# A graph network kernel with a hand-written issue order: block work spread over iterations, weight scaling on ScalarE, thresholds on GpSimd, single PSUM banks

## The chip, the cores and the metric

One core of one Trainium2 chip. The metric is the device time of one execution in microseconds; lower is better. Every kernel timed here gave a correct result. All medians and ranges quoted are of runs labelled "fast". Three kernels had one run each labelled "slow", being over 1.5% above the fastest of the same kernel; it is left out. Engines are named as in the profile: PE is TensorE, PEld its weight loads, DVE is VectorE, ACT is ScalarE, POOL is GpSimd.

## The reference

128 graphs of 64 nodes with 128 features. For every edge (i, j) of the adjacency matrix a three-layer perceptron runs on the pair of features; the messages are summed by node and a second perceptron updates the node.

```python
def _mlp(x, w0, b0, g0, be0, w1, b1, g1, be1, w2, b2):
    h = _layernorm(relu(x @ w0 + b0), g0, be0)
    h = _layernorm(relu(h @ w1 + b1), g1, be1)
    return h @ w2 + b2

messages = _mlp(concat(f_i, f_j), msg_...) * adj[..., None]     # (128, 64, 64, 128)
agg      = sum(messages, axis=2)
updated  = x + _mlp(concat(x, agg), upd_...)                    # cut: names shortened
```

About an eighth of the pairs are edges, so the kernel packs the edges first. It works in 160 iterations of 512 edges; ten iterations are one block of eight graphs, and four of ten iterations also sum a pair of graphs.

## The kernel before

"Node marks" are five matmuls that write a 128x128 tile each into PSUM; each half of a tile is then scaled by the reciprocal standard deviation of its edges (the "weights"), and `reduce` uses them as the stationary operand.

```python
ps_z = es.enter_context(tc.tile_pool(name="ps_z", bufs=2, space=PSUM))
ps_y = es.enter_context(tc.tile_pool(name="ps_y", bufs=1, space=PSUM))
ps_m = es.enter_context(tc.tile_pool(name="ps_m", bufs=2, space=PSUM))
def bank():
    return ps_m.tile([P, 512], F32, name="ms")
# ... (cut)
def make_tp(p):
    tp = tpp.tile([P, CAP], F16, name="tp")
    nc.vector.tensor_scalar(tp, slot, cumall[:, p:p + 1], None, op0=ALU.is_lt)
# ... (cut)
def weights(p):
    q, h = divmod(p, 2)
    w = wp.tile([P, TG, 2, N], F32, name="w")
    qv = Q[q][:, h * 2 * TG:(h + 1) * 2 * TG].rearrange("p (g t) -> p t g", g=2)
    for t0, t1 in ((0, CH), (CH, TG)):
        ps = bank()
        for t in range(t0, t1):
            nc.tensor.matmul(ps[:, (t - t0) * P:(t - t0 + 1) * P],
                             lhsT=TP[p][:, t * P:(t + 1) * P],
                             rhs=pick.rearrange("p g m -> p (g m)"), start=True, stop=True)
        nt = t1 - t0
        nc.vector.tensor_tensor(w[:, t0:t1], ps[:, 0:nt * P].rearrange(...),
                                qv[:, t0:t1].unsqueeze(3).to_broadcast([P, nt, 2, N]),
                                op=ALU.mult)                       # cut: one argument shortened
```

PSUM is the memory that the matmuls write to. A tile of 512 f32 columns in it is called a bank here; a pool with `bufs=2` has two banks and hands them out anew when they have been read.

Names in the profile, in the order of the work: `tp` are the thresholds and `mk` the marks of the edges, which the compare turns into the selection `s`; `hps` and `h` are the first layer, `hT` is h transposed for its statistics `st`; `z` is the second layer's product, `sdb` what is added to it, `y` its output; `w` are the weights and `ys` the sum over edges. `um...`, `uh`, `uy` and `usdb` are their counterparts in the update of the nodes, `xn` and `ysum` its inputs; `abh` and `abl` are a high and a low part of the first layer's products by node.

Marks and weights stand in one function, so a bank is filled and read at once. The block's other work (transposes, layer products of the update) comes from generators that a scheduler interleaves.

## Time and profile before

| | before |
|---|---|
| median of 3 runs, first measurement | 772.11 us |
| span of the profiled run, mean granted clock | 769.7 us, 0.956 |
| PE busy, DVE busy | 654.7 us (85%), 673.4 us (87%) |
| one block (ten iterations), from the y rows | 44.3 us |

"Busy" is the union of an engine's instructions. The mean granted clock is the share of full speed at which TensorE was let run. The lines behind these numbers stand in the prediction.

### The profile page before, as it was taken

To read this page: it belongs to the slowest core of one execution; us is meant where nothing else is said; L and a number is where in the kernel's file an instruction comes from. 1 tells how busy PE (TensorE), PEld (TensorE's weight loads), DVE (VectorE), ACT (ScalarE), POOL (GpSimd) and SP (SyncE) were. 2 spreads that over 40 slices of the span, in tenths; PEclk is the share of its full clock that TensorE was granted. 3 is DMA by queue.
4 is the path that set the end of the run, shared out by engine and by line. 5 is a ranking of instruction groups with operands and counts; after the bars stand their busy time and mean duration, and the time that the engine had idled before them with its cause. 6 is when DMAs were issued, how large, how long until landed. Compare 5 with 4: busy or idle time off the path is not lost.

```text
span 769.7 us, 15357 instructions
## 1 busy us (share of the span) xinstructions
PE 654.7 (85%) x5667; PEld 558.6 (73%) x5667; DVE 673.4 (87%) x2397; ACT 208.0 (27%) x402; POOL 366.1 (48%) x651
## 2 busy tenths in 40 slices
PE   2688899898898979889898988889799898989773
PEld 2567778687777868778786877778687787878663
DVE  7678998988888999898998989989989898999872
ACT  1143232232232223223322323222232233222111
POOL 6346345444354454545455454545545354435531
PEclk9699999999899999999999999989999999999997
DMA  5000000100001010000101000010000000000000
GB/s 137 1 21 8 3 8 1 35 1 24 12 2 36 1 30 7 15 22 1 35 3 35 1 17 14 1 29 1 29 1 16 1 1 14 1 15 2 14 15 16
DMA packets 27883, 12.04 MB, mean 16 GB/s; under 512 B 10391, under 2 KB 27805, under 8 KB 27805
## 3 DMA queue, kind: packets, MB, share of 16 engines
q1 hardware_dynamic: 26496, 11.01, 5.1%
q8 instruction: 46, 0.75, 0.4%
q14 instruction: 33, 0.26, 0.1%
q10 hardware_dynamic: 1308, 0.01, 0.1%
HBM read 6.82 MB, written 4.19 MB: 14 GB/s over the span
## 4 chain that ended last, share of the span: by engine, by line
PE 48%; DVE 36%; POOL 10%; issue 2%; ACT 2%; DMA 1%; ACTq 0%; POOLq 0%; DVEq 0%
PE z L435 8%; PE ys L476 7%; DVE st L446 7%; PE ms L504 7%; PE hps L410 7%; DVE s L401 7%; PE hT L420 5%; DVE st L424 5%; PE mk L396 4%; PE ms L358 3%; DVE y L234 3%; POOL xo L488 3%; PE ms L494 2%; DVE uo L538 2%; POOL sdb L429 2%
## 5 line engine op out<-in xcount | busy, mean ns | idle before, releaser
L429 POOL TENSOR_TENSOR sdb<-b1b,m_sd 128x512 f32<-128x512 f32 x160 | 168.1, 1052 | 194.4 <-DVE y L234 136.0
L435 PE MATMUL z<-w1c,h 128*128 128x128 f32 x1280 | 201.3, 288 | 2.9 <-DVE y L234 2.5
L413 ACT ACTIVATE h<-hps,b0c 128x512 f32<-128x512 f32 x160 | 110.1, 688 | 311.8 <-PE hps L410 308.4
L435 PEld LDWEIGHTS z<-w1c,h 128*128 128x128 f32 x1280 | 173.4, 197 | 16.0 <-DVE y L234 7.6
L424 DVE BATCH_NORM_STATS2 st<-hT 128x6 f32<-128x128 f32 x640 | 147.4, 283 | 4.1 <-PE hT L420 3.9
L446 DVE BATCH_NORM_STATS2 st<-y 128x6 f32<-128x128 f32 x640 | 137.4, 278 | 0.0
L401 DVE TENSOR_TENSOR s<-mk,cmpt 128x512 fp32r<-128x512 f32 x160 | 109.4, 684 | 15.9 <-PE mk L396 14.8
L410 PE MATMUL hps<-s,abl 128*128 128x512 f32 (+3 forms) x256 | 101.9, 408 | 18.1 <-DVE s L401 17.7
L420 PE MATMUL hT<-ident,h 128*128 128x128 f32 x640 | 104.8, 288 | 6.6 <-DVE st L424 6.2
L234 DVE CUSTOM_DVE_ANT_0 y<-z,sdb 128x512 f32<-128x512 f32 x160 | 107.9, 676 | 1.3 <-POOL sdb L429 1.3
L396 PE MATMUL mk<-tp,qs 128*128 128x512 f16 (+3 forms) x256 | 66.4, 312 | 38.6 <-DVE s L401 30.1
L420 PEld LDWEIGHTS hT<-ident,h 128*128 128x128 f32 x640 | 75.2, 146 | 24.3 <-DVE st L424 18.7
L476 PE MATMUL ys<-y,w 128*64 128x128 f32 x1280 | 91.0, 281 | 1.8 <-DVE w L461 1.8
L476 PEld LDWEIGHTS ys<-y,w 128*64 128x64 f32 x1280 | 73.2, 139 | 14.9 <-issue 10.2
L410 PE MATMUL hps<-s,abh 128*128 128x512 f32 (+3 forms) x256 | 81.8, 336 | 0.0
L410 PEld LDWEIGHTS hps<-s,abl 128*128 128x128 f32 x256 | 51.6, 202 | 26.8 <-DVE s L401 20.2
L396 PEld LDWEIGHTS <-qs 128*128 128x128 f16 x256 | 25.1, 100 | 58.8 <-issue 57.0
L461 DVE TENSOR_TENSOR w<-ms,m_q 128x512 f32<-128x512 f32 (+1 forms) x128 | 61.0, 479 | 0.4 <-PE ms L456 0.4
L410 PEld LDWEIGHTS hps<-s,abh 128*128 128x128 f32 x256 | 52.0, 203 | 0.9
L240 POOL TENSOR_TENSOR m_d<-st 128x20 f32<-128x20 f32 x64 | 15.9, 248 | 73.8 <-DVE st L424 52.1
L244 DVE SCALAR_TENSOR_TENSOR m<-m_d,m_s 128x20 f32<-128x20 f32 x64 | 11.5, 179 | 32.0 <-POOL m_d L241 29.9
L488 POOL TENSOR_TENSOR xo<-xn,cu2b 128x512 f32<-128x512 f32 x16 | 20.5, 1282 | 34.3 <-DVE uo L538 33.3
(162 smaller groups left out, 939.1 us busy)
## 6 DMA issues: line engine op xcount, KB each, us to landing
xn<-in_x_dram SPq DMA_DIRECT2D x16, 256.0 KB, 2.8
out_dram<-uo SPq DMA_DIRECT2D x16, 256.0 KB, 2.3
an<-in_adj_dram SPq DMA_DIRECT2D x16, 128.0 KB, 2.2
w<-in_L_gnn_msg_w_dram SPq DMA_DIRECT2D x2, 64.0 KB, 2.3
u<-in_L_gnn_upd_w_dram SPq DMA_DIRECT2D x2, 64.0 KB, 2.1
w0a<-in_L_gnn_msg_w_dram SPq DMA_DIRECT2D x1, 64.0 KB, 1.8
w0b<-in_L_gnn_msg_w_dram SPq DMA_DIRECT2D x1, 64.0 KB, 2.4
u0a<-in_L_gnn_upd_w_dram SPq DMA_DIRECT2D x1, 64.0 KB, 2.3
```

Of the source, the lines that this page charges most:

```text
L234: nc.vector._custom_dve(TENSOR_ADD_SAT, out=o, in0=ps, in1=sb, s0=BIG, s1=0.0)
L396: nc.tensor.matmul(ps[:, at:at + w], lhsT=blocks[g // (2 * PB)]["qs"][:, g // 2 % PB, g % 2, :], rhs=TP[g // 2][:, e:e + w], start=True, s ...
L401: nc.vector.tensor_tensor(s, ps, cmpt[:, o:o + CH * P], op=ALU.is_equal)
L410: nc.tensor.matmul(ps[:, at:at + w], lhsT=ab[:, g % 4, :], rhs=s[:, at:at + w], start=(k == 0), stop=(k == 1))
L413: nc.scalar.activation(h, ps, AF.Relu, bias=b0c)
L420: nc.tensor.transpose(ps[:, t, :], H[n][:, t * P:(t + 1) * P], ident)
L424: nc.vector.bn_stats(ST0[q][:, CH * c + t, :], ps[:, t, :])
L429: nc.gpsimd.tensor_tensor(sdb, bc(W["b1b"], CH), SD[q][:, CH * c:CH * c + CH].unsqueeze(2).to_broadcast([P, CH, C]), op=ALU.mult)
L435: nc.tensor.matmul(ps[:, t, :], lhsT=h[:, t * P:(t + 1) * P], rhs=W["w1c"], start=True, stop=True)
L446: nc.vector.bn_stats(ST1[q][:, CH * c + t, :], Y[n][:, t, :])
L461: nc.vector.tensor_tensor(w[:, t0:t1], ps[:, 0:nt * P].rearrange("p (t g m) -> p t g m", t=nt, g=2), qv[:, t0:t1].unsqueeze(3).to_broadcas ...
L476: nc.tensor.matmul(YS[b][g * N:(g + 1) * N, k, :], lhsT=w[:, t, g, :], rhs=y, start=(t == 0), stop=(t == TG - 1))
```

## The change

The intent: VectorE and TensorE were both nearly full, and TensorE could do its work in about 36 us per block. So VectorE is relieved (weights to ScalarE, thresholds and small variance steps to GpSimd), and each piece of block work gets a fixed iteration and place, in an order that the framework may not alter. The core of the diff, cut:

```diff
-        ps_z = es.enter_context(tc.tile_pool(name="ps_z", bufs=2, space=PSUM))
+        ps_z = es.enter_context(tc.tile_pool(name="ps_z", bufs=1, space=PSUM))
-        ps_m = es.enter_context(tc.tile_pool(name="ps_m", bufs=2, space=PSUM))
+        ps_a = es.enter_context(tc.tile_pool(name="ps_a", bufs=2, space=PSUM))   # abank(), "ma"
+        ps_u = es.enter_context(tc.tile_pool(name="ps_u", bufs=1, space=PSUM))   # ubank(), "mu"
-            nc.vector.tensor_scalar(tp, slot, cumall[:, p:p + 1], None, op0=ALU.is_lt)
+            nc.gpsimd.tensor_scalar(tp, slot, cumall[:, p:p + 1], None, op0=ALU.is_lt)
+        def node_marks(p):
+            WT[p] = []
+            for t in range(TG):
+                if t % 4 == 0:
+                    ps = abank()
+                WT[p].append(ps[:, t % 4 * P:(t % 4 + 1) * P])
+                nc.tensor.matmul(WT[p][t], lhsT=TP[p][:, t * P:(t + 1) * P], ...)
         def weights(p):
-                nc.vector.tensor_tensor(w[:, t0:t1], ps..., qv..., op=ALU.mult)
+            for t in range(TG):
+                for g in range(2):
+                    nc.scalar.activation(w[:, t, g, :], WT[p][t][:, g * N:(g + 1) * N], AF.Copy,
+                                         scale=Q[q][:, k:k + 1])
+            at(u - 1, "e", bias0, b)              # GpSimd, two instructions
+            at(u + 1, "x", turn, b, "ysum")       # PE: four transposes into abank()
+            at(u + 5, "a", upd_root0, b)          # ACT: um_sd, from a GpSimd result
+            at(u + 5, "x", turn, b, "uh")         # PE, abank()
+            at(u + 6, "a", turn_out, b, "uh")     # ACT copies that bank
+            at(u + 8, "x", turn, b, "uy")         # PE, abank()
+            at(w, "x", node_marks, p)             # PE fills two abanks
+            at(w + 1, "r", weights, p)            # ACT reads them, one iteration later
+            at(w + 2, "x1", reduce, p)
+        es.enter_context(tc.manual_schedule())
```

Within an iteration the places come in the order a, (compare, statistics), m, (layer 1, layer 0 with `h` on ACT), r, x, x1, x2, (marks of the next iteration), e.

## The prediction

> **What bounds the kernel now.** I read the page's busy shares first. Columns: busy us, share of the span, instructions.
>
> ```profile
> PE 654.7 (85%) x5667; PEld 558.6 (73%) x5667; DVE 673.4 (87%) x2397; ACT 208.0 (27%) x402; POOL 366.1 (48%) x651
> ```
>
> The shares include the start and the end, so next the table of stretches. Columns: stretch, span, then busy and count of PE, PEld, DVE, ACT, POOL, then the clock.
>
> ```profile
> 200.00:300.00 100.00, 88.65 (x791) 76.17 (x788) 89.50 (x322) 29.55 (x58) 47.87 (x86) 0.98 0.05 14
> 400.00:500.00 100.00, 87.90 (x784) 75.21 (x783) 92.11 (x337) 29.48 (x58) 50.81 (x93) 0.98 0.05 13
> ```
>
> VectorE (DVE) is over 90% busy on average and TensorE (PE) close to 90%: two engines are nearly full, each waiting for the other. Which of them is truly full, only a dense piece tells. PE, in the timeline (start, duration, operation):
>
> ```profile
> 421.65 0.60 PE L420 MATMUL hT<-ident,h 128*128 128x128 f32 x4
> 422.09 0.83 PE L435 MATMUL z<-w1c,h 128*128 128x128 f32 x6
> 422.76 0.60 PE L333 MATMUL ms<-pos,dq 128*128 128x256 f32 x2
> 423.29 1.31 PE L476 MATMUL ys<-y,w 128*64 128x128 f32 x20
> 424.53 0.66 PE L348 MATMUL ms<-ident,xn 128*128 128x128 f32 x4
> 425.03 0.38 PE L396 MATMUL mk<-tp,qs 128*128 128x512 f16 x1
> ...
> 425.76 0.62 PE L420 MATMUL hT<-ident,h 128*128 128x128 f32 x4
> ```
>
> From start to start: four transposes hT 0.44 us, a z pass 0.11, the dq product 0.53, a whole ys reduction 1.24, a block transpose 0.50, marks and both hps products together 0.73. Durations overlap; starts are what counts. Between such pieces PE waits for DVE, as the list of waits says (total, times, longest):
>
> ```profile
> PE mk L396 <- DVE s L401: 30.1, 43, 1.0
> PEld hT L420 <- DVE st L424: 18.7, 33, 1.5
> POOL sdb L429 <- DVE y L234: 136.0, 79, 3.5
> ```
>
> So DVE sets the pace and PE fills its gaps. A loop iteration handles 512 edges; there are 160, ten per block. The y rows of the timeline start at 90.5 us (the tenth) and 710.7 (the 150th): 44.3 us per block.
>
> **What the Trainium skill says.** "Trainium Kernel Development and Optimization", section Best Practices: judge TensorE not by matmul busy time. The trace agrees: six z passes "last" 0.83 us but the next work starts after 0.67. "GPSIMD Engine Reference", section 4.1: two-input elementwise work is about twice slower there than on VectorE, one-input work roughly at line rate, PSUM out of reach. The trace has 1052 ns for the two-input 512-column sdb and 615 ns for the f16 copy of 512; so the thresholds (one input, SBUF) can go to GpSimd, and the weights (PSUM) only to ScalarE. "VectorE: DVE Perf Modes", section What auto-detection actually checks: the packed mode wants every tensor 16-bit. In s the PSUM operand stays f32, so cmpt in f16 should leave s at its 684 ns. "PSUM — Partial Sum Buffer", section on bank collisions: guard by bank. With one z bank, z of the next iteration waits for y of this one; before, two banks hid that.
>
> **The change part by part.** Off DVE (lines of the groups by form: busy us, mean ns):
>
> ```profile
> L461 DVE TENSOR_TENSOR w<-ms,m_q 128x512 f32<-128x512 f32 x64 | 43.6, 681 | 0.4 <-PE ms L456 0.4
> L376 DVE TENSOR_SCALAR tp<-slot,cumall 128x640 f16<-128x640 f16 x64 | 26.3, 417 | 0.0
> L461 DVE TENSOR_TENSOR w<-ms,m_q 128x128 f32<-128x128 f32 x64 | 17.7, 276 | 0.0
> L314 DVE COPY deg<-rk 128x4 f32<-128x4 f32 x16 | 10.3, 644 | 0.0
> L244 DVE SCALAR_TENSOR_TENSOR m<-m_d,m_s 128x20 f32<-128x20 f32 x64 | 11.5, 179 | 32.0 <-POOL m_d L241 29.9
> ```
>
> That is 109 us; with the small variance steps and copies (L244 for blocks, L250, L258, L312, L343) about 137, or 8.5 per block; about 8 as a union. DVE then has per iteration, by starts, s 0.60, four statistics 0.80, y 0.60, four more 0.77 = 2.77, and per block 6.5 of other work: 34 us per block.
>
> PE does the same products: per iteration z 0.90, hT 0.44, marks and hps 0.75-0.8, say 2.15; per four graph pairs 4 x (1.24 + 0.30 for node marks) = 6.1; per block 8.2 (two row steps of 1.0, dq 0.5, counts 0.25, four transposes 1.8, 32 layer passes of 0.11). Sum 35.8 per block. A perfect schedule is therefore PE bound at 36 us against 44.3.
>
> ScalarE (ACT) gets the weights: 64 x 10 instructions of 128x64. Its 20-column root takes 219 ns, its 512-column h 688, so about 0.26 us each, perhaps 0.2 by starts: 2 to 2.6 us in four iterations of ten, 8 to 10 per block. ACT goes to some 22 us per block, not full.
>
> GpSimd (POOL) gets the thresholds, an estimate of 0.9 us each from the 615 ns copy, and some six further small instructions per variance, now chained, each 0.2 to 0.3 us. It goes from 23 to about 30 us per block, on one strictly ordered queue. The existing pieces:
>
> ```profile
> L429 POOL TENSOR_TENSOR sdb<-b1b,m_sd 128x512 f32<-128x512 f32 x160 | 168.1, 1052 | 194.4 <-DVE y L234 136.0 <-ACT m_sd L252 35.1 <-DVE um L244 22.3
> L486 POOL TENSOR_TENSOR m<-m,ub0b 128x512 f32<-128x512 f32 x16 | 20.4, 1276 | 1.3
> L484 POOL TENSOR_TENSOR m<-c2u,deg 128x512 f32<-128x512 f32 x16 | 16.6, 1040 | 18.4 <-DVE c2u L218 11.4 <-DVE uh L234 5.2
> L320 POOL TENSOR_TENSOR pos<-rk,before 128x256 f32<-128x256 f32 x16 | 9.8, 612 | 1.2
> ```
>
> Here I see the new bound. In the changed program one iteration of each ten (call it j2) puts on POOL, in this order: the variance of y, which waits for DVE's last statistics of that iteration (1.7 us), the two bias instructions (2.35), the placement of the next block, eight instructions (4.6), a threshold (0.9), and only then sdb for y two iterations later (1.1): 10.65 us in a row. PE and DVE have some 7 us of work until they need that sdb, and single banks let neither run ahead. So the period of a block is a chain: 10.65 on POOL; 0.65 from that y to the next z; seven PE iterations, 3.7 + 4.4 + 4.4 + 2.9 + 3.05 + 4.7 + 2.85 = 26.0; then z, y and statistics, 2.45. Sum 39.75. The clock of 0.97 on 26 us adds 0.8, small waits (h coming late from ACT in short iterations) 0.5: 41.0 per block. ACT's worst place, a layer product in j2 that waits for the copy behind ten weights, loses about 0.7 us, but inside POOL's shadow.
>
> The sum: first y 56.5 us before; I put 52, as the preparation of later blocks no longer crowds the start. 159 intervals of 4.10: 652. The first and last blocks are lighter: before, 159 x 4.43 = 704 against 683 real (56.5 to 739.7), so minus 20. From the last y to the end, 30 us before: 28, a chain of latency that the change does not shorten. 52 + 652 - 20 + 28 = 712 us.
>
> **The rivals.** First, no POOL backlog: sdb comes in time because the two bias instructions and the placement are quicker or slip into waits. Then PE is the bound at 36 to 37.5 per block, and the time is about 655. For it speaks POOL's mean load, 30 of 41; against it the strict order. Second, ACT: if a weight instruction costs 0.35 us rather than 0.2 to 0.26, ten of them fill an iteration, h comes late everywhere, and PE waits in four iterations of ten: 43 per block, about 740. For it speaks the single bank for h; against it ACT's present 27%. Third, the hand order loses what the scheduler found: each iteration pays a handoff PE to DVE and back, 0.2 to 0.3 us in ten places, which also gives about 740, and with a slow threshold instruction (2 us) no gain at all.
>
> **Range and chances.** The chain gives 712; 655 without the backlog I hold at one in six; 740 at one in six; no gain at one in twelve. A range of 665 to 746 should hold it 8 times in 10. The 2% line lies at 756.7, so faster 0.90, same 0.08, slower 0.02.
>
> **What would show it.** In the page after: DVE busy about 540 us, ACT about 370, POOL about 480. In the waits: DVE y waiting for POOL sdb, some 3 us, 16 times; w instructions of 0.2 to 0.26 us; thresholds of 0.9 us on POOL; s unchanged near 684 ns. In the timeline: PE dense from start to start in most iterations, with one gap of about 3 us per block before a z. I am wrong if y never waits for sdb (then 655), or if PE waits for h behind weights (then 740).

## More of the kernel before

One more view: the list of waits for the two shared banks, named `ms` (engine, tile and line, what it waited for, total us, times, longest).

```profile
PE ms L311 <- DVE rk L306: 8.0, 12, 0.7
PE ms L333 <- POOL pos L322: 7.4, 3, 3.7
PE ms L494 <- DVE uy L234: 3.5, 2, 2.0
```

Apart from two single waits at the start (10.2 and 4.9 us), these are PE's largest before a matmul into a shared bank: about 19 us in the whole run.

## The result, and the profile after

The changed kernel took **837.13 us** (four runs, 833.2 to 837.62), the kernel before 772.32 us beside it (four runs). The ratio is 1.0824, 95% interval 1.0788 to 1.086. Ratios here are the mean time of one kernel's fast runs over that of the other's of the same rounds, so not quite the ratio of the medians quoted. All outputs are right. The span of the profiled run was 835.4 us, the mean granted clock 0.924.

The page's busy row, and the table of stretches (stretch, span, then busy and count of PE, PEld, DVE, ACT, POOL, then granted clock, DMA share, GB/s):

```profile
PE 658.4 (79%) x5667; PEld 572.7 (69%) x5667; DVE 585.8 (70%) x1975; ACT 341.0 (41%) x1074; POOL 546.6 (65%) x1003
```

```profile
200.00:300.00 100.00, 83.25 (x763) 73.55 (x762) 75.92 (x259) 44.35 (x143) 72.15 (x132) 0.93 0.05 14
400.00:500.00 100.00, 81.66 (x723) 71.77 (x724) 74.49 (x252) 44.58 (x145) 69.00 (x126) 0.91 0.05 14
```

VectorE was relieved, from about 90% to 75% busy in the middle, but TensorE fell as well, and it does fewer matmuls in each stretch (723 against 784 in the second). Both engines now wait. So something between them holds both up. The groups of moved work, by form (busy us, mean ns of one, idle before):

```profile
L451 POOL TENSOR_SCALAR tp<-slot,cumall 128x640 f16<-128x640 f16 x64 | 120.5, 1883 | 0.0
L547 ACT ACTIVATE w<-ma,m_q 128x64 f32<-128x64 f32 x640 | 137.3, 344 | 2.2 <-PE ma L536 1.8 <-DVE m_q L281 0.4
```

A threshold takes 1.88 us on GpSimd; it took 0.417 on VectorE. And the list of waits:

```profile
PE ma L412 <- ACT w L547: 79.7, 43, 2.5
ACT um_sd L262 <- POOL um L256: 77.9, 16, 7.8
PE ma L536 <- ACT uhT L418: 40.1, 15, 4.0
DVE y L245 <- POOL sdb L504: 36.1, 16, 2.5
```

The fourth line is the wait that the prediction named, 16 times, at three quarters of its size. The first and third are new and stand on TensorE: 119.8 us, or 7.5 us per block, before matmuls whose *data* are ready but whose PSUM *bank* is not free. How this comes about shows in the timelines of PE and ACT over one stretch (start, duration, operation, idle before and what ended it):

```profile
411.15 0.28 PE L482 MATMUL hps<-s,abh 128*128 128x128 f32 x1
413.84 0.82 PE L412 MATMUL ma<-ident,ysum 128*128 128x128 f32 x4 [2.41 <-ACT w L547]
414.45 1.06 PE L398 MATMUL ma<-pos,dq 128*128 128x256 f32 x2
...
432.32 0.39 PE L536 MATMUL ma<-pick,tp 128*128 128x128 f16 x4
435.26 0.27 PE L536 MATMUL ma<-pick,tp 128*128 128x128 f16 x1 [2.55 <-ACT uhT L418]
435.32 0.63 PE L467 MATMUL mk<-tp,qs 128*128 128x512 f16 x1
435.75 1.06 PE L491 MATMUL hT<-ident,h 128*128 128x128 f32 x4
```

```profile
411.46 0.69 ACT L485 ACTIVATE h<-hps,b0c 128x512 f32<-128x512 f32 x1 [2.52 <-PE hps L482]
412.05 2.15 ACT L547 ACTIVATE w<-ma,m_q 128x64 f32<-128x64 f32 x10
...
433.18 0.30 ACT L262 ACTIVATE um_sd<-um,eps_c 128x4 f32<-128x4 f32 x1 [4.66 <-POOL um L256]
433.38 0.57 ACT L435 CAST abh<-mu 128x512 fp32r<-128x512 f32 x1
433.85 0.31 ACT L276 ACTIVATE m_sq<-m_v,eps_c 128x20 f32<-128x20 f32 x1
434.06 0.67 ACT L485 ACTIVATE h<-hps,b0c 128x512 f32<-128x512 f32 x1
434.63 0.58 ACT L418 COPY uhT<-ma 128x512 f32<-128x512 f32 x1
```

PE ends the hps products at 411.43 and comes to the transposes of ysum. They want one of the two `ma` banks, and both still hold node marks from the iteration before. ScalarE reads those only after `h`, and `h` waits for the very hps just made: 0.69 us of h, then eight weight instructions that empty the first bank. The sum is the 2.41 us gap. In the iteration at 432 the fifth node mark wants the bank in which the turned uh lies; ScalarE copies that only in the next iteration, behind um_sd, which waits 4.66 us for GpSimd. In each case the marks of the next iteration stand behind the blocked matmul in TensorE's fixed order, so VectorE's compare waits too (80.5 us in the whole run for `mk`; 14.8 before the change).

The bank is not all of that second wait. The next transposes of h (L491, at 435.75) read an h that stood behind the same um_sd and ended at 434.73. With a free bank TensorE would have come to them and waited for that h, so about 1.0 us of the 2.55 is the bank's alone (an estimate from these two times); the rest is ScalarE's blocked queue.

Slow matmuls follow both gaps. dq (L398) took 1.06 us behind the first; it took 0.60 before the change. The transposes of h took 1.06 at 435.75; elsewhere in the same stretch 0.60. The granted clock was 0.55 from 414 to 416 us and 0.50 from 435 to 437. Behind the gap before 448.81, also 2.41 us, it stayed at 1.00.

### The profile page after: what moved, and what is told of

It is laid out like the page before. It is cut to its first block, busy times and chain, and to the rows that moved or that the text cites. A ratio compares the mean times of both kernels' runs of the same rounds, so it can differ in the third digit from the quotient of the medians.

```text
span 835.4 us, 15966 instructions
## 1 busy us (share of the span) xinstructions
PE 658.4 (79%) x5667; PEld 572.7 (69%) x5667; DVE 585.8 (70%) x1975; ACT 341.0 (41%) x1074; POOL 546.6 (65%) x1003
## 4 chain that ended last, share of the span: by engine, by line
PE 48%; POOL 17%; DVE 16%; ACT 14%; issue 3%; DMA 1%; ACTq 0%; DVEq 0%; POOLq 0%
PE z L513 13%; ACT w L547 7%; PE hps L482 6%; PE hT L491 6%; PE ys L560 6%; PE mk L467 4%; PE mu L589 4%; ACT h L485 4%; PE ma L412 4%; DVE y L245 3%; DVE st L520 3%; DVE st L495 2%; POOL tp L451 2%; DVE s L474 2%; PE mu L426 2%
## 5 line engine op out<-in xcount | busy, mean ns | idle before, releaser
L504 POOL TENSOR_TENSOR sdb<-b1b,m_sd 128x512 f32<-128x512 f32 x160 | 164.6, 1038 | 84.7 <-ACT m_sd L262 84.7
L513 PE MATMUL z<-w1c,h 128*128 128x128 f32 x1280 | 186.2, 292 | 9.6 <-DVE y L245 8.4
L474 DVE TENSOR_TENSOR s<-mk,cmpt 128x512 fp32r<-128x512 f32 x160 | 109.2, 682 | 80.8 <-PE mk L467 80.5
L495 DVE BATCH_NORM_STATS2 st<-hT 128x6 f32<-128x128 f32 x640 | 141.4, 285 | 4.3 <-PE hT L491 4.3
L245 DVE CUSTOM_DVE_ANT_0 y<-z,sdb 128x512 f32<-128x512 f32 x160 | 107.4, 671 | 50.3 <-POOL sdb L504 36.1
L547 ACT ACTIVATE w<-ma,m_q 128x64 f32<-128x64 f32 x640 | 137.3, 344 | 2.2 <-PE ma L536 1.8
L451 POOL TENSOR_SCALAR tp<-slot,cumall 128x640 f16<-128x640 f16 x64 | 120.5, 1883 | 0.0
L491 PE MATMUL hT<-ident,h 128*128 128x128 f32 x640 | 111.5, 303 | 7.4 <-ACT h L485 7.4
L491 PEld LDWEIGHTS hT<-ident,h 128*128 128x128 f32 x640 | 86.2, 157 | 30.6 <-ACT h L485 13.9
L482 PE MATMUL hps<-s,abl 128*128 128x512 f32 (+3 forms) x256 | 96.2, 386 | 0.0
L560 PE MATMUL ys<-y,w 128*64 128x128 f32 x1280 | 87.1, 284 | 0.0
L536 PE MATMUL ma<-pick,tp 128*128 128x128 f16 x320 | 32.2, 225 | 40.1 <-ACT uhT L418 40.1
```

The source lines that it names most:

```text
L245: nc.vector._custom_dve(TENSOR_ADD_SAT, out=o, in0=ps, in1=sb, s0=BIG, s1=0.0)
L451: nc.gpsimd.tensor_scalar(tp, slot, cumall[:, p:p + 1], None, op0=ALU.is_lt)
L474: nc.vector.tensor_tensor(S[n], MK.pop(n), cmpt[:, o:o + CH * P], op=ALU.is_equal)
L482: nc.tensor.matmul(ps[:, c:c + w], lhsT=ab[:, g % 4, :], rhs=s[:, c:c + w], start=(k == 0), stop=(k == 1))
L491: nc.tensor.transpose(ps[:, t, :], H[n][:, t * P:(t + 1) * P], ident)
L495: nc.vector.bn_stats(ST0[q][:, CH * c + t, :], ps[:, t, :])
```

## The experiments

Eighteen kernels ran, each timed in three rounds. The kernel before had medians from 769.83 to 772.14 us beside them, so medians may be compared within a few us. Numbers given as "+32" are differences of medians in us. "Its mark" is what the text before the run had put for an outcome. The four repairs used are:

- **early weights**: ScalarE reads the marks at the end of the iteration that made them;
- **um**: um_sd behind `h`, and the copy of the turned uh at the end of its own iteration;
- **thresholds** on VectorE again;
- **bias**: the update's two bias instructions on GpSimd moved behind the placing of the next block.

### Single repairs of the changed kernel

**e1_early_w** takes away the first wait.

```diff
-            at(w + 1, "r", weights, p)
+            at(w, "e", weights, p)
```

> The changed kernel, with one edit: the ten ScalarE weight instructions of a graph pair are issued at the end of the iteration in which TensorE made their node marks, not behind h of the next one. Theory A (two PSUM banks are held by the node marks until ScalarE has read them, and the block transposes behind them wait): the 43 waits of ma L412 for w, 79.7 us, fall to under 20 us, and the time falls by 50 to 70 us from 837, to about 775. Theory B (GpSimd backlog, thresholds of 1.88 us): sdb comes as late as before, the wait of y for sdb grows into the place of the other, and the time falls by under 20 us, to 820 or more.

Measured: 841.04 us (836.18 to 848.56), ratio 1.0986 to before: a small loss where 50 to 70 us of gain were expected, and no theory had put one. The transposes' wait on the weights is gone from the list, but two others have come:

```profile
PE ma L536 <- ACT w L547: 62.8, 15, 5.7
PE mk L467 <- POOL tp L451: 52.7, 15, 3.8
```

The fifth node mark now waits, up to 5.7 us, until ScalarE has read the first four marks of its *own* pair: it starts at 427.66, when eight weight instructions (425.86 to 427.61) have emptied the bank. They are late because ScalarE's queue still stands at um_sd (78.0 us, 16 times, in this run too). Early weights behind a blocked queue are not early.

**e2_tp_dve** puts the thresholds back on VectorE.

```diff
-            nc.gpsimd.tensor_scalar(tp, slot, cumall[:, p:p + 1], None, op0=ALU.is_lt)
+            nc.vector.tensor_scalar(tp, slot, cumall[:, p:p + 1], None, op0=ALU.is_lt)
```

> The changed kernel with the thresholds back on VectorE (64 instructions of about 0.42 us instead of 1.88 us on GpSimd), nothing else. Theory B (GpSimd backlog): 7.5 us per block leave GpSimd, the wait of y for sdb (36 us) goes, and the time falls by 30 us or more, to 805 or less. Theory A (banks): the transposes still wait for w, 75 to 90 us, and the time changes by under 15 us.

Measured: 826.09 us, 11 less, as theory A expected. y's wait for sdb falls from 36.1 to 2.9 us, but the bank waits stay (79.2 and 40.9).

**e4_um** takes ScalarE's queue off um_sd.

```diff
-            at(u + 5, "a", upd_root0, b)
+            at(u + 5, "r", upd_root0, b)
-            at(u + 6, "a", turn_out, b, "uh")
+            at(u + 5, "e", turn_out, b, "uh")
```

> The changed kernel with two ScalarE instructions of the block update moved: the root um_sd behind h of its iteration, and the copy of the turned uh to the end of the iteration of its transpose instead of the next one. Theory C (ScalarE stands in order behind um_sd, which waits 4.7 us per block for GpSimd, and with it the bank for the fifth node mark): the 15 waits of ma L536 for uhT, 40 us, fall under 10 us, and the time falls by 30 to 45 us, to about 800. If TensorE has only moved to another wait (the y chain over GpSimd), under 15 us.

Measured: 813.56 us, 24 less, between its marks (30 to 45, or under 15). um_sd's wait fell from 77.9 to 8.1, the fifth node mark's from 40.1 to 22.9; the wait on the weights grew to 88.4.

**g3_bias** moves only the bias.

```diff
-            at(u - 1, "e", bias0, b)
+            at(u + 2, "e", bias0, b)
```

> The changed kernel with only the update's bias (2.3 us on GpSimd) moved behind the placing of the degrees. Hidden behind the bank waits: under 15 us gained, 822 us or more. If GpSimd's queue is on the path beside the banks: 40 us or more gained, as taking this repair out of the best version cost 45.

Measured: 831.67 us, 5 less, as "hidden" expected; the intervals of the two ratios overlap, so even the 5 is not clear of noise.

**e6_w_dve** takes ScalarE out of the weights: two multiplications on VectorE as before the change, ahead of y in the iteration behind the marks. The diff is cut: a second edit keeps whole banks in `WT`.

```diff
-            at(w + 1, "r", weights, p)
+            at(w + 1, "m", weights, p)
-                    nc.scalar.activation(w[:, t, g, :], ..., scale=Q[q][:, k:k + 1])
+                nc.vector.tensor_tensor(w[:, t0:t1], ps..., qv..., op=ALU.mult)
```

> The changed kernel with the weights back on VectorE (two products per pair, 0.68 and 0.28 us), issued ahead of y in the iteration after the node marks; the banks are handed over in the same iteration as before but after 2.2 us of it instead of about 5. Theory A (banks held): the transposes hardly wait any more, TensorE's 80 us fall under 20, time about 775. If ScalarE's own load or the order alone were the cause, not the banks, VectorE's 50 us more would be felt and the time would stay above 815.

Measured: 816.98 us, 20 less. By its marks this is a miss for the banks (about 775) and fell, by 2 us, on the side of ScalarE's load or the order (above 815). The list of waits says why little was gained: the transposes now wait for VectorE in place of ScalarE, nearly as long (`PE ma L412 <- DVE w L547`, 74.9 us, up to 4.8). In the one stretch looked at, at 402.34 us, the multiplications stood behind nball (L391), which waits for GpSimd. So a late reader holds the bank on VectorE too.

**e3_auto** leaves out the line that fixes the order and lets the framework choose it.

```diff
-        es.enter_context(tc.manual_schedule())
```

> The changed program without its fixed order: the line that switches the scheduler off is taken out, so the scheduler orders the same instructions with the same engines, buffers and banks. If the hand order is the cause (theories A and C both need it: block work is put where the banks are held), the scheduler finds fillers and the time is at or below the 772 of the kernel before. If the placing of work (thresholds of 1.88 us on GpSimd, ten small weight instructions on ScalarE, single banks) is the cause, it stays above 810.

Measured: 854.84 us, 18 *more*. The same pieces in an automatic order are slower still; a loss from hand ordering as such is not the cause (three of the four repairs below are moves within the hand order). The two bank waits are nearly gone in this run (2.8 us on L536, none on L412 for w). In their place TensorE waits for late work of ScalarE elsewhere: 62.6 us for `w` before the sum over edges, 51.0 us for `h`, which empties the single hps bank.

### Each named move done to the kernel before

**b1_w_act** (the weights as ten ScalarE instructions) and **b2_tp_pool** (the thresholds on GpSimd) do one part of the change alone on the kernel before.

```diff
 b1:
-                nc.vector.tensor_tensor(w[:, t0:t1], ps..., qv..., op=ALU.mult)
+                for t in range(t0, t1):
+                    for g in range(2):
+                        nc.scalar.activation(w[:, t, g, :], ..., AF.Copy, scale=qv[:, t, g:g + 1])
 b2:
-            nc.vector.tensor_scalar(tp, slot, cumall[:, p:p + 1], None, op0=ALU.is_lt)
+            nc.gpsimd.tensor_scalar(tp, slot, cumall[:, p:p + 1], None, op0=ALU.is_lt)
```

> The kernel before, with its scheduler, and the weights alone moved to ScalarE (640 instructions of about 0.34 us in place of 128 on VectorE). If the move itself is bad (banks held for 2 us instead of 0.8), slower than 772 by 2% or more. If it is good and only the order around it bad, VectorE loses 51 of its 673 us and the time falls to 730 to 750.

> The kernel before, with its scheduler, and the thresholds alone moved to GpSimd (1.88 us each instead of 0.42 on VectorE). GpSimd goes from 366 to about 485 us busy. If the thresholds are harmful by themselves, they delay sdb and the time rises above 780; if they are harmless, VectorE loses 19 us by starts and the time falls to 755 to 765.

Measured: b1 759.49 us, ratio 0.9859 (0.983 to 0.9888): a gain of 1.4%, clear of noise but under the 2% at which a kernel counts as faster, and short of its mark of 730 to 750. b2 795.68 us, ratio 1.0328 (1.0295 to 1.0361): a loss, above its mark of 780, with the same cost of an instruction, in the groups of b2:

```profile
L376 POOL TENSOR_SCALAR tp<-slot,cumall 128x640 f16<-128x640 f16 x64 | 120.4, 1882 | 24.3 <-PE ms L456 19.7 <-DVE cumall L312 4.6
```

The threshold on GpSimd costs time in both kernels. The weights on ScalarE cost none where the marks are read at once.

### All repairs together, and each left out

**e5_all** has all four.

> The changed kernel with weights issued in the iteration of their node marks, thresholds on VectorE, the two ScalarE moves of the update, and the two bias instructions on GpSimd moved three iterations later, away from the placement of the next block. If banks, the um_sd order and the GpSimd backlog together are what holds TensorE, its waits vanish and a block nears its 36 us of dense TensorE work: 38 to 40 us per block, 670 to 700 us in all. If something not yet seen binds, above 740.

Measured: **704.45 us**, ratio 0.9121 (0.9084 to 0.9158) to before, 133 below the changed kernel and just above its mark of 670 to 700. The busy row and the stretches:

```profile
PE 609.8 (87%) x5667; PEld 533.6 (76%) x5667; DVE 611.1 (87%) x2039; ACT 343.7 (49%) x1074; POOL 430.6 (61%) x939
```

```profile
200.00:300.00 100.00, 89.98 (x892) 80.27 (x891) 94.84 (x313) 53.70 (x168) 65.87 (x147) 1.00 0.05 15
400.00:500.00 100.00, 90.00 (x892) 80.31 (x891) 95.27 (x316) 53.37 (x169) 66.32 (x148) 1.00 0.06 15
```

892 matmuls in a stretch in place of 723 to 763, and the granted clock is 1.00 where it was 0.91 to 0.93. The same 5667 matmuls were busy 609.8 us, not 658.4. The span fell by 132.2 us; 48.6 of that is shorter busy time of PE and 83.6 shorter idle time (835.4 - 658.4 = 177.0 against 703.2 - 609.8 = 93.4). VectorE is at 95% in the stretches: it is again the fullest engine.

Then each repair was taken out of it: **f1_no_tp** (thresholds on GpSimd), **f2_no_early** (late weights), **f3_no_um** (um as in the change), **f4_no_bias** (bias as in the change). The edits are those above, undone.

> e5_all with the thresholds left on GpSimd (1.88 us each), the other three edits kept. The single edits took at most 24 us off 837, all four together 133. If the thresholds on GpSimd are the part that holds all the rest, this run goes back above 790; if the banks are, it stays under 730.

> e5_all with the weights left behind h of the next iteration, as in the changed kernel. Theory A (banks held into the next iteration): the waits of ma L412 for w, about 75 us, come back and the time rises by 60 us or more, to 765 or above. If GpSimd was the real cause and the bank waits only stood in its shadow, under 720.

> e5_all without the two ScalarE moves of the update. Theory C: the wait of the fifth node mark for uhT, 24 us in e5_all, goes back to 40 us or more and the time to 720 to 740. If the moves matter only with a late GpSimd, 700 to 712.

> e5_all with the two bias instructions back in the iteration of the placement. The prediction's chain on GpSimd (variance, bias, placement, then sdb) is then whole but without the threshold: the wait of y for sdb, 7.5 us in e5_all, rises by up to 2 us per block, and the time by 15 to 30 us, to 720 to 735. If GpSimd has slack there once the thresholds are gone, under 712.

| repair | alone on the changed kernel | taken out of e5_all | wait that came back |
|---|---|---|---|
| early weights | 841.04 (+4) | 778.99 (+75) | PE L412 on ACT w, 80.5 us |
| um | 813.56 (-24) | 767.22 (+63) | PE L536 on ACT w, 63.4 us |
| bias | 831.67 (-5) | 749.25 (+45) | PE z on DVE y, 42.1 us |
| thresholds | 826.09 (-11) | 736.56 (+32) | DVE y on POOL sdb, 23.2 us, and PE mk on POOL tp, 15.1 us |

f2 met its mark (765 or more). f1 fell between its two (790, 730). f3 and f4 cost more than theirs (720 to 740, 720 to 735), and other waits came back than the ones named.

Alone the four gain 36 us in sum (with early weights' loss counted); taken out, they cost 215 in sum; together they are worth 133. This fits waits that lie behind one another in strictly ordered queues: with one removed, the work runs into the next. The lines of f2 and f3 that show two of them:

```profile
PE ma L412 <- ACT w L547: 80.5, 43, 3.1
```

```profile
PE ma L536 <- ACT w L547: 63.4, 15, 5.7
```

**g2_early_um** has early weights and um only, on the changed kernel.

> The changed kernel with early weights and um's evictions moved, thresholds still on GpSimd. Waits that hide one another: alone the first lost 8 us and the second gained 24, together at least 50 gained, 787 us or less. If the gains only add: about 820.

Measured: 792.18 us (788.1 to 794.63), 45 below the changed kernel, where +4 and -24 would add to 20 (the text has a loss of 8, from the median with the slow run). It missed its own mark of 787 by a little, but lies far from the 820 of simple adding. What is left in its list of waits is GpSimd's:

```profile
PE mk L467 <- POOL tp L451: 44.6, 15, 3.8
DVE y L245 <- POOL sdb L504: 37.0, 17, 2.5
```

From here bias gives 56 more (f1, 736.56), thresholds 43 (f4, 749.25), both 88 (e5). So with most of the bank waits gone the kernel is still slower than the one before, and the larger gain then comes from GpSimd's queue. The counterpart, both GpSimd repairs without the other two, was not run.

### Is it the banks? Other banks with the order unchanged

**e7_turn_u** keeps every instruction and place of the changed kernel and turns ysum, uh and uy into the `mu` bank. **e8_turn_u_tp** adds the thresholds on VectorE.

```diff
-            blk[src + "_ps"] = abank()
+            blk[src + "_ps"] = abank() if src == "xn" else ubank()
```

> The changed kernel with only the PSUM bank of the turned ysum, uh and uy altered: same instructions, same places. Theory A (TensorE is held because the transposes share two banks with the node marks, which wait for ScalarE's ten weight instructions): the waits of the transposes on the weights fall from 79.7 us to about 25 (the turned xn, which keeps the old bank), the fifth node mark's wait on the copy of uh (40.1 us) goes, and the time falls by 40 us or more, to 795 us or less. Rival B (the hand order and ScalarE's own work set the pace): the time stays within 15 us of 837. Rival C (GpSimd's thresholds take over): the bank waits go, but the mask or y's wait on GpSimd grows from 36 us to 60 or more, and less than 25 us is gained.

> The one before with the thresholds on VectorE as well. Theory A with hidden waits: more than the 11 us that this move gained alone, 20 to 40 us below the run with the bank alone, 765 us or less. Rival: the two gains only add as single ones, 11 us below it or no gain.

Measured: e7 823.61 us, e8 806.6 (805.11 to 816.11): 14 and then 17 less, a miss for the bank theory as it was put. By its marks e7 fell to rival B, the hand order and ScalarE's own work; e8's 17 lies between its two. The list of waits of e7 shows why little was gained:

```profile
PE mu L412 <- DVE abl L442: 43.0, 26, 2.8
PE ma L398 <- POOL a L387: 24.1, 12, 2.0
PE ma L357 <- ACT w L547: 15.2, 12, 1.3
PE ma L412 <- ACT w L547: 10.8, 14, 2.5
```

The fifth node mark's wait is gone. But right behind the turned ysum stands the step product (L398), and behind the turned uy the count (L357), both in the old banks. They wait in the transposes' place. For L398 the profile names GpSimd as the releaser, but the timelines of e7, PE first and then ACT, say otherwise:

```profile
403.53 0.63 PE L412 MATMUL mu<-ident,ysum 128*128 128x128 f32 x4
406.16 1.08 PE L398 MATMUL ma<-pos,dq 128*128 128x256 f32 x2 [2.00 <-POOL a L387]
```

```profile
404.32 2.15 ACT L547 ACTIVATE w<-ma,m_q 128x64 f32<-128x64 f32 x10
```

L398 starts 1.84 us after the first weight instruction; in the changed kernel the transposes of ysum started 1.79 us after theirs (413.84 - 412.05). GpSimd's `a`, the named releaser, was over at 405.71 and is not an input of this product. So the bank wait was handed on to the next matmul, and a new one came with the other bank: the turned uh waits there for abl (2.78 us at 428.60), whose copy abh stands behind um_sd in ScalarE's queue.

**g1_late_u** asks the same with the other three repairs in place: late weights, the other bank for the three.

> Thresholds on VectorE, um's evictions and the update's bias moved, the weights late as in the changed kernel, and the turned ysum, uh and uy in the other bank. If the bank is what the late weights cost: most of the 75 us that the early weights were worth come back, 725 us or less (779 without the other bank, 704 with early weights). If the late weights cost through ScalarE's queue (h or the copies behind them): 765 us or more. The turned xn still uses the old banks, so some 16 waits of about 1 to 2.5 us stay.

Measured: 770.22 us (763.93 to 775.33), 9 below f2 (the intervals of the ratios overlap) and not the 54 hoped for; by the number it lies where "ScalarE's queue" was expected. In its timeline too the step product waits 2.00 us, in the iteration of the turned ysum, until 1.84 us after the first weight instruction. A kernel with the turned xn in the other bank as well, so that fewer users share the marks' banks, could not be run: a deadlock, which can be followed in the program. The turned xn would wait until VectorE has read the product of `layer` out of the same bank, and VectorE comes to that only after a compare whose marks stand behind these transposes on TensorE.

**e9_all_u** adds the other bank to all four repairs.

> All four repairs plus the other bank for the turned blocks. If the remaining wait of the fifth node mark (23.7 us in the version with all four) is on the path: 685 to 698 us. If VectorE (87% busy there) has become the bound: within 6 us of 704.

Measured: **690.33 us** (687.43 to 691.26), ratio 0.8981 (0.8929 to 0.9033): faster than both kernels, and within its mark of 685 to 698. The fifth node mark's last 23.7 us of waits are gone; 20.4 us of waits for the other bank (`PE mu L412 <- DVE abl L442`) have come. Its stretches:

```profile
200.00:300.00 100.00, 93.37 (x907) 82.52 (x908) 95.42 (x327) 56.76 (x182) 70.57 (x157) 1.00 0.07 18
400.00:500.00 100.00, 92.60 (x906) 81.14 (x901) 94.93 (x322) 56.03 (x181) 69.83 (x150) 1.00 0.08 21
```

A block takes 38.5 us (y rows: 81.4 for the tenth, 620.4 for the 150th, over 14).

## Why the prediction was wrong

It said 712 us (665 to 746) and faster; it was 837 and slower. Its sums are right as sums. Point by point:

- **The two ends of the machine: right.** VectorE was relieved and ScalarE has room (busy 341.0 us; 370 was put). s stayed at 682 ns. Weight instructions start every 0.2 us (ten in 2.15 us), as put; the 0.344 us of one is overlap. VectorE's busy time fell to 585.8, not 540: the removed rows sum to 137 us, but busy is a union of instructions that overlap, so taking rows away shortens it by less.
- **GpSimd's chain: right in kind and nearly in size.** Predicted 10.65 us from the variance to the sdb behind the threshold; the chain of waits has 11.1 (405.20, first variance step, to 416.32, end of sdb). The threshold's term was mis-sized, 0.9 against 1.88 us, and 64 x 0.98 = 63 us is nearly the whole excess of POOL's busy time (546.6 against 480); in the chain, shorter steps elsewhere took half of it back, so that the total came out near is in part luck. y waited for sdb 16 times, 2.3 us each where 3 was said. The chain's two ends and its y:

```profile
405.20 0.25 POOL L252 TENSOR_TENSOR m_d<-st 128x20 f32<-128x20 f32 x1 [1.06 <-DVE st L520]
415.27 2.03 POOL L504 TENSOR_TENSOR sdb<-b1b,m_sd 128x512 f32<-128x512 f32 x2
452.99 0.25 POOL L252 TENSOR_TENSOR m_d<-st 128x20 f32<-128x20 f32 x1 [1.07 <-DVE st L520]
```

```profile
416.34 0.69 DVE L245 CUSTOM_DVE_ANT_0 y<-z,sdb 128x512 f32<-128x512 f32 x1 [2.46 <-POOL sdb L504]
```

- **The step that failed: "seven PE iterations, 3.7 + 4.4 + 4.4 + 2.9 + 3.05 + 4.7 + 2.85 = 26.0".** It adds starts of matmuls as if each found its PSUM bank free. The bank rule was cited, and used for z alone. For the node marks I saw that marks and weights were parted by one iteration and did not ask what else draws from the same two banks in between, nor how late ScalarE's queue would come to read them. From one GpSimd chain to the next the trace has 47.8 us (405.20 to 452.99). Less 11.1 that is 36.7 us; predicted were 0.65 + 26.0 + 2.45, with 0.8 and 0.5 for clock and small waits 30.4. In this stretch PE waited for banks 0.63 (turned xn), 2.55 (fifth node mark) and 2.41 us (turned uy): 5.6 of the 6.3 missing. (The 2.41 us before 413.84 lay inside the GpSimd chain.) I put the other 0.7 down to the slower clock behind the gaps, 0.50 from 435 to 437 us and 0.82 to 440 where 0.97 was put; it was not measured apart. About 1.5 of the 2.55 would have been lost to the late h as well.

```profile
425.02 0.66 PE L412 MATMUL ma<-ident,xn 128*128 128x128 f32 x4 [0.63 <-ACT w L547]
448.81 0.66 PE L412 MATMUL ma<-ident,uy 128*128 128x128 f32 x4 [2.41 <-ACT w L547]
```

- **The sum then closes, but taking these waits away does not give it back.** The first y came at 56.4 (52 was put), first to last y took 738.8 (632), the tail 40.2 (28): 835.4. Of the 107 us in the middle, 6.7 a block make nearly all. Why the tail grew by some 10 us was not tested. In g2, which takes the waits of the transposes for the weights away, 792.18 us remain, 80 above the 712: other waits come out, for the thresholds (44.6 us), for the count's input rk (25.9 us) and still for the fifth node mark (22.9 us), and the clock in the two stretches is 0.91 and 0.92. So the free banks are the step that failed in the kernel as it ran, and the mis-sized threshold is a second error that stands behind it.
- **The rivals.** "ACT late, 740" was nearest: PE did wait behind the weights, yet mostly through the banks and less through `h`, and in three iterations per block with 0.6 to 2.4 us. "The hand order loses" did not hold as the cause: without it e3 is slower still; but its slow threshold of 2 us, with "no gain at all", came true in the threshold (1.88). "PE bound at 36 to 37.5, about 655" is what the program comes near when the waits are mostly gone: 38.5 and 690.33 in e9, with VectorE at 95%. I gave losing more than 2% a chance of 0.02, since no rival ended above the old time; none had two waits adding up.

**What is shown and what is not.** Shown: PE's bank waits on late readers, that they exist with the reader on either engine (e6), that e5 cuts them from 119.8 us to 23.7 and wins, that both the late reads and GpSimd's queue cost time there (each repair taken out costs 32 to 75 us), and that the repairs depend on one another (the table and g2). Not settled: how the 75 us of the late weights divide between the bank and ScalarE's queue. The two tests meant for that moved the wait to the next user of the bank, and the version that would have parted them cannot run.

## What to carry to other kernels

When a PSUM tile's writer and reader are moved into different iterations, list everything that draws from the same pool between them, on the writer's engine: in a strict order the first of these stops all that follows. Count the span from fill to the last read as the bank's use, with everything that stands ahead of the reader in its own queue. And when one repair gains little, don't drop it: take it out of a version that has all repairs before judging.

## What the Trainium skill lacked or had wrong

- "GPSIMD Engine Reference", section 4.1 Engine selection, has one-input work on GpSimd at roughly line rate. The threshold (one tensor input, f16, 128x640, a comparison with a per-partition number) took 1883 ns there and 417 ns on VectorE in the kernel before, 4.5 times as long. From its start to that of GpSimd's next instruction it was the same: 461.20 to 463.06 us in the changed kernel. The f16 copy of 512 columns took 610 ns on GpSimd, so this holds for the comparison and not for every one-input instruction.
- "TensorE: Matmul & The Clock Gate", Part 1, puts the fall to the cold clock after an idle window of about 3.4 us, and further down tells of short idles at PSUM banks that made the clock swing, without a length for them. Here gaps of 2.41 and 2.55 us were followed by matmuls of 1.06 us in place of 0.60, and two other gaps of 2.41 us (before 401.02 and 448.81) were not. The mean granted clock in the stretches was 0.91 to 0.93 in the changed kernel and 1.00 in e5 and e9. The page's free-running window may account for the difference; no run here tells.
- "PSUM — Partial Sum Buffer", bank collisions: it says to guard by bank, but not what a guard costs when the reader is late. Here TensorE waited 119.8 us. "Perfetto Trace Analysis", section Optimization Strategy, has the sign for it (a gap that repeats can mean too few buffers), and the trace agrees with the sign: 2.41 us before 401.02, 413.84 and 448.81. More banks alone were no cure: another bank for three of the users gained 14 us (e7).
- No page looked at says that a wait moves to the next user of the bank when one user is taken away (e7: 24.1 us on L398, 15.2 on L357), nor that repairs of ordered queues don't add (36 us alone, 133 together).
